# Seams of a four-layer graph network: six row buffers and deferred adds at the end of four-head attention, a routed layer's stores and row numbers, and other queues for readbacks

## The chip, the cores and the metric

The kernel runs on one core of a Trainium2 chip. The core has five engines that run side by side: TensorE (PE) multiplies matrices and transposes tiles, VectorE (DVE) and ScalarE (ACT) work element by element, GpSimd (POOL) does some setup and issues DMAs, SyncE (SP) issues DMAs. The metric is the device time of one launch in microseconds (us); lower is better.

## The reference, cut to what matters

A graph of 2,708 nodes with 256 features each passes through four layers. Each layer adds a graph step and a feed-forward step to X, each on the layer-normed X. All is fp32.

```python
x = x + L0_gnn(layernorm(x), adj, ...)   # cosine attention on the graph
x = x + L0_ffn(layernorm(x), ...)        # attention over slices
x = x + L1_gnn(layernorm(x), adj, ...)   # four-head graph attention
x = x + L1_ffn(layernorm(x), ...)        # eight experts, the best one per node
x = x + L2_gnn(layernorm(x), adj, ...)   # single-head graph attention
x = x + L2_ffn(layernorm(x), ...)        # a decoder block; two of its experts per node
x = x + L3_gnn(layernorm(x), adj, ...)   # single-head graph attention, ELU
x = x + L3_ffn(layernorm(x), ...)        # linear

def L1_gnn(x, adj, W, a1, a2):
    h = (x @ W).reshape(n, 4, 64)
    si, sj = einsum('nhd,d->nh', h, a1), einsum('nhd,d->nh', h, a2)
    e = where(adj > 0, leaky_relu(si[:, None] + sj[None], 0.2), -9e15)
    return einsum('ijh,jhd->ihd', softmax(e, axis=1), h).reshape(n, 256)

def L1_ffn(x, W1, b1, Wg, bg, Wd, bd):
    H = gelu(x @ W1 + b1)                      # 1,024 wide
    probs = softmax(H @ Wg + bg)               # 8 experts
    assign = argmax(probs)
    return sum over e of (assign == e) * probs[e] * (H @ Wd[e] + bd[e])
```

## The kernel before

The nodes lie in 22 tiles of 128 rows (the last has 20), X stays on the chip as 128 x 22 x 256, and a "block" is up to 512 nodes, four tiles; there are six blocks, the last of two tiles. `net_kernel` (L2014) calls the layers in turn. Most of the order on an engine follows from the order in which the code issues, with a scheduler between; `tc.issue_after(x)` pins an instruction behind another on its engine.

**Four-head attention**, `gat_heads` (L678). The heads go in two pairs. For each source tile j, ACT (L674) and DVE (L675) make the weights e of both heads against all nodes; TensorE adds values into six accumulators `acc` (L780, one PSUM bank each) and the sums of weights into `den` (L788, one bank). After the 22 tiles of a pair, DVE copies den to `ds` (L798), TensorE turns it (L801), DVE makes the reciprocals `rd` (L803, L806). Then, block by block, acc goes to a row buffer `o` of which there are three (L810, ACT and DVE in turn), is turned by TensorE into the one PSUM bank `aux` (L815), multiplied by rd (`y`, L822) and added to X (L829). `mark_empty` (L2049) loads two rows of flags into the mask by ACT's DMA queue (L2053, L2054), ahead of the pair loop.

**The top-1 layer**, `top1_ffn` (L857), has three stages.
- Its head: eight expert weights `wd` of 1 MB each are loaded by SP (L880), `ln_stats` takes layer norm's sums and roots for all tiles in groups of four (L96; a group is `bn_stats` L144, `bn_aggr` L145, ACT's square root L147, DVE's reciprocal L151), and w (1 MB, L892) comes by GpSimd's queue.
- Its hidden part, over the blocks: `features` (L894) norms and turns four tiles, `hidden` (L904) multiplies by w (L911) and applies GELU on ACT, `gate` (L932) computes logits and a rank for each node and lets GpSimd scatter each tile's 128 node numbers, four bytes each, into lists in DRAM called `fnodes` (L1444). `store` (L918) turns the hidden rows back (L926), copies them to row buffers `hr` (three, DVE and ACT in turn, L927) and lets SP write them to DRAM, `hidden` (L930). The stores of the last two blocks both follow the last gate.
- Its expert part: SP loads the node numbers as columns, 128 x 8 for the first eight tiles (L1554, `load_first`) and 128 x 1 for each later one (L1550, `load`); DVE casts them to integers (L980); GpSimd fetches each tile's rows of `hidden` (L990); TensorE turns them (L1003) and multiplies by wd (L1035); the result goes out by GpSimd (`send`, L1573).

`Routing.combine` (L1583) reads the experts' results back into y by SP's and ACT's queues in turn (L1594) and adds them to X (L1604). It runs at the start of the single-head layer and of the last graph layer, whose mask `reload_graph` (L2057) clears by GpSimd and loads again by SP, with `mark_empty` behind it.

Of the kernel before, what the change touches and what calls it, by code (L numbers as in the profile page):

```python
# [677 lines left out]
def gat_heads(net):  # L678
# [8 lines left out]
    Q = len(cols) // 2  # L687
    with ExitStack() as ctx:
        big = ctx.enter_context(tc.tile_pool(name="g1big", bufs=1))
        V = big.tile([P, NT, H, DH], F32, name="V")  # L690
        ratio = big.tile([P, NT, H], F32, name="ratio")

        low = big.tile([P, NT, H, 2 * Q - 1], F32, name="low")
        big_p = big.tile([P, H, N], F32, name="big_p")
# [73 lines left out]
        for p in range(2):  # L768
# [3 lines left out]
            nc.tensor.matmul(den, zero, big_p[0:1, 0, :512], start=True, stop=False, skip_group_check=True)  # L772
            for j in range(NT):
                e = wide.tile([P, 2, N], F32, name="e")
                for k, h in enumerate(heads):
                    gat_pairs(net, e[:, k, :], j, 0, N, big_p[:, h, :], ratio[:, j, h : h + 1])
                for n, (i0, iw) in enumerate(cols):
                    for k, h in enumerate(heads):
                        half = slice(k * DH, (k + 1) * DH)
                        nc.tensor.matmul(  # L780
                            acc[n][half, :iw], V[:, j, h, :], e[:, k, i0 : i0 + iw], start=j == 0, stop=j == NT - 1
                        )
                for q in range(Q):
                    for k, h in enumerate(heads):
                        for half in range(2):
                            i0, iw = cols[half * Q + q]
                            g = (2 * k + half) * 32
                            nc.tensor.matmul(  # L788
# [6 lines left out]
                            )  # L795

            ds = small.tile([P, 512], F32, name="ds", bufs=1)
# [4 lines left out]
            rd = small.tile([P, 4, 4, Q], F32, name="rd", bufs=1)  # L802
# [4 lines left out]
            out = []  # L807
            for n, (i0, iw) in enumerate(cols):
                o = small.tile([P, 512], F32, name="o", bufs=3)
                (nc.vector.tensor_copy if n % 2 else nc.scalar.copy)(o[:, :iw], acc[n][:, :iw])  # L810
                pt = paux.tile([P, 4, P], F32, name="aux")
                its = tiles_of(i0, iw)
                for c, i in enumerate(its):
                    r = rows(i)
                    nc.tensor.transpose(pt[:r, c, :], o[:, c * P : c * P + r], net.ident)  # L815
                whole = [c for c, i in enumerate(its) if rows(i) == P]
                for c0, c1, r in [(0, len(whole), P)] + [(c, c + 1, rows(its[c])) for c in range(len(whole), len(its))]:
                    nt = c1 - c0
                    y = small.tile([P, 4, 2, DH], F32, name="y")

                    d = rd.rearrange("p c (k b) q -> p c k b q", b=2)[:r, c0:c1, :, n // Q, n % Q]
                    nc.vector.tensor_tensor(  # L822
                        y[:r, :nt],
                        pt[:r, c0:c1, :].rearrange("p c (k d) -> p c k d", d=DH),
                        d.unsqueeze(3).to_broadcast([r, nt, 2, DH]),
                        ALU.mult,
                    )
                    xs = X[:r, its[0] + c0 : its[0] + c1, p * 2 * DH : (p + 1) * 2 * DH]
                    nc.vector.tensor_tensor(xs, xs, y[:r, :nt].rearrange("p c k d -> p c (k d)"), ALU.add)  # L829
# [27 lines left out]
def top1_ffn(net, ctx):  # L857

    nc, tc, a, X = net.nc, net.tc, net.a, net.X
    E, HID = 8, 1024
    KC = HID // P
    with ExitStack() as inner:
        big = ctx.enter_context(tc.tile_pool(name="f1big", bufs=1))
        dram = ctx.enter_context(tc.tile_pool(name="f1dram", bufs=1, space=bass.MemoryType.DRAM))
        wd = inner.enter_context(tc.tile_pool(name="f1wd", bufs=1, side="right")).tile([P, E, KC, D], F32, name="wd")
# [11 lines left out]
        for e in range(E):  # L879
            nc.sync.dma_start(wd[:, e], a["f1_wd"][e].rearrange("(c p) m -> p c m", p=P))  # L880
        route = Routing(net, big, dram, 1, "f")
        ln = net.ln_stats()
# [3 lines left out]
        with tc.tile_pool(name="f1tp", bufs=2, space=PSUM) as ptp, tc.tile_pool(  # L886
# [7 lines left out]
            def features(its):  # L894
                ft = work.tile([P, 2, 512], F32, name="ft")
                for k, t in enumerate(its):
                    r = rows(t)
                    f = rp.tile([P, D], F32, name="f", bufs=2)
                    net.normed(f, t, ln)
                    ps = net.transposed(ptp, f, r)  # L900
                    nc.vector.tensor_copy(ft[:, :, k * P : k * P + r], ps[:, :, :r])
                return ft

# [14 lines left out]
            def store(its, halves):  # L918

                for k, t in enumerate(its):  # L920
                    r = rows(t)
                    for n, half in enumerate(halves):
                        hr = rp.tile([P, 512], F32, name="hr", bufs=3)
# [3 lines left out]
                        (nc.scalar.copy if n else nc.vector.tensor_copy)(  # L927
# [21 lines left out]
            blocks, kept = chunks(512), []  # L949
            ft = features(tiles_of(*blocks[0]))  # L950
            for n, (n0, nw) in enumerate(blocks):
                its = tiles_of(n0, nw)
                halves = hidden(ft, nw)
                if n + 1 < len(blocks):
                    ft = features(tiles_of(*blocks[n + 1]))
                gate(its, halves, nw)
                kept.append((its, halves))
                if n + 2 != len(blocks):
                    for k in kept:
                        store(*k)  # L960
                    kept.clear()
        route.finish()
        prep = ctx.enter_context(tc.tile_pool(name="g2prep", bufs=1))
        with tc.tile_pool(name="f1t", bufs=1, space=PSUM) as pt, tc.tile_pool(
# [5 lines left out]
            node, number, to = (  # L970
                sp.tile([P, route.tiles], t, name=name, bufs=1)
                for t, name in ((F32, "node"), (I32, "number"), (I32, "to"))
            )
# [40 lines left out]
            for s in range(E, usual):  # L1014
                route.load(s, node[:, s : s + 1])
# [1143 lines left out]
```

## Time and profile before

| | us |
|---|---|
| median of three runs (2892.7 to 2900.67) | 2898.42 |
| the profiled execution | 2896.45 |
| its span | 2894.7 |
| four-head attention, from den of the first pair's first tile (707.75) to the last pair's last den (1070.06) | 362.3 |
| from there to the first matmul of the hidden part, L911 (1095.19) | 25.1 |
| hidden part to the first expert matmul (1251.88) | 156.7 |
| last store of `hidden` issued | 1231.8 |
| last graph layer: readbacks issued (2576.82) to TensorE's first transposes (2597.47) | 20.7 |

The times in brackets are microseconds from the start of the span. The profile's page gives each engine's busy time; the window view gives, for a stretch, the busy time of each engine with its instruction count, TensorE's granted clock (1.00 is full), the share of the DMA engines in use and the GB/s that they moved. A timeline line is the start, the duration, the engine (with a q for the engine's DMA-issuing queue) and line, the operation, what it writes and reads, and in square brackets how long the engine had been idle before it and what released it. A waits line gives engine and instruction, what it waited for, the total, the number of waits and the longest.

### The profile page before, as it was taken

The page shows a single profiled execution, that of the slowest core. Times are in us where ns is not written, and L with a number is a line of the kernel's source. Part 1 is how long each engine was busy: PE and PEld are TensorE (multiplying, and loading weights), DVE is VectorE, ACT ScalarE, POOL GpSimd, SP SyncE. Part 2 cuts the span into 40 slices and gives each one's busy share as a digit, 9 for nine tenths or more (in the row PEclk, how much of TensorE's full clock was granted, in tenths as well). Part 3 has the DMA queues.
Part 4 walks back from the last instruction along what each step waited for, and adds up shares of the span by engine and source line. Part 5 has one row for each costly group of instructions (what it writes and reads, how often), then busy time and mean ns, then how long its engine had stood idle before and what let it go on. Part 6 is the DMA issues. An engine that isn't in the chain of part 4 may idle for free. (4 is left out here: it accounts for less than half of the span.)

```text
span 2894.7 us, 32765 instructions
## 1 busy us (share of the span) xinstructions
PE 2651.2 (92%) x11893; PEld 1624.4 (56%) x11893; DVE 1441.4 (50%) x3062; ACT 1041.2 (36%) x1658; POOL 369.5 (13%) x462
## 2 busy tenths in 40 slices
PE   6999989799999989878899899998979999969998
PEld 5667746563333334567688433333346677747885
DVE  7753358344777774432644455455543222235455
ACT  3344433224665643211543223233312222215453
POOL 0000012100000001133300123223321111110002
PEclk9999999698999998989999999899969999989999
DMA  8899210000000005354200100002021111041001
GB/s 298 280 292 312 104 65 1 8 1 1 1 1 1 1 19 173 91 166 130 87 1 0 34 22 17 15 0 93 15 101 41 34 30 34 28 137 59 1 1 39
DMA packets 113729, 197.70 MB, mean 68 GB/s; under 512 B 12380, under 2 KB 71636, under 8 KB 110732
## 3 DMA queue, kind: packets, MB, share of 16 engines
q1 hardware_dynamic: 92758, 147.89, 16.1%
q0 software_dynamic: 13120, 38.06, 4.0%
q10 hardware_dynamic: 7690, 9.62, 1.1%
q8 instruction: 99, 1.62, 0.2%
q14 instruction: 62, 0.51, 0.1%
HBM read 135.82 MB, written 59.71 MB: 68 GB/s over the span
## 5 line engine op out<-in xcount | busy, mean ns | idle before, releaser
L675 DVE SCALAR_TENSOR_TENSOR e<-e,mask 128x768 f32<-128x768 f32 (+2 forms) x264 | 411.7, 1574 | 310.9 <-ACT e L674 310.7
L674 ACT ACTIVATE e<-big_p,minus_one,ratio 128x768 f32<-128x768 f32 (+2 forms) x264 | 394.9, 1513 | 363.4 <-PE acc L1236 229.8
L1236 PE MATMUL acc<-V,e 128*128 128x257 f32 (+1 forms) x1936 | 433.5, 383 | 4.5 <-DVE e L675 4.4
L1236 PEld LDWEIGHTS acc<-V,e 128*128 128x128 f32 (+1 forms) x1936 | 352.3, 186 | 85.7 <-issue 32.1
L780 PE MATMUL acc<-e,V 128*64 128x512 f32 (+1 forms) x1056 | 249.7, 550 | 4.1 <-DVE e L675 4.1
L1878 PE MATMUL h<-w,ft 128*128 (+1 forms) x752 | 233.0, 452 | 0.5 <-ACT ft L1860 0.5
L284 PE MATMUL acc<-F,e 128*128 128x257 f32 x968 | 226.3, 384 | 3.3 <-DVE e L281 2.9
L284 PEld LDWEIGHTS acc<-F,e 128*128 128x128 f32 x968 | 173.4, 185 | 67.3 <-DVE e L281 28.7
L780 PEld LDWEIGHTS acc<-e,V 128*64 128x64 f32 x1056 | 95.4, 137 | 180.6 <-issue 159.0
L1719 PE MATMUL sc<-qt,kt 64*128 64x512 f32 (+4 forms) x656 | 187.0, 535 | 4.1 <-ACT e L1729 2.4
L1729 ACT ACTIVATE e<-sc 128x1024 f32<-128x1024 f32 (+4 forms) x140 | 102.8, 760 | 204.5 <-PE sc L1719 188.4
L1878 PEld LDWEIGHTS h<-w,ft 128*128 128x128 f32 x752 | 136.0, 191 | 56.7 <-issue 1.4
L281 DVE TENSOR_TENSOR e<-e,mask 128x512 f32<-128x512 f32 (+2 forms) x132 | 80.4, 625 | 149.4 <-ACT e L275 147.8
L1737 DVE TENSOR_TENSOR sum<-sum,e 128x1024 f32<-128x1024 f32 (+4 forms) x102 | 103.8, 1018 | 99.1 <-ACT e L1729 97.4
L275 ACT ACTIVATE e<-score 128x512 f32<-128x512 f32 (+2 forms) x132 | 69.7, 544 | 179.2 <-PE score L273 153.0
L1734 PE MATMUL po<-e,V 128*64 128x512 f32 (+5 forms) x560 | 119.4, 511 | 14.8 <-ACT e L1729 8.8
L1910 PE MATMUL po<-w,ht 114*128 (+1 forms) x564 | 129.5, 379 | 0.9 <-DVE ht L1903 0.9
L1719 PEld LDWEIGHTS sc<-qt,kt 64*128 64x128 f32 x656 | 71.8, 198 | 94.8 <-issue 80.9
L788 PE MATMUL den<-e,low 128*3 128x512 f32 (+1 forms) x1056 | 123.1, 542 | 0.0
L1910 PEld LDWEIGHTS po<-w,ht 114*128 114x128 f32 x564 | 106.7, 189 | 22.6 <-DVE ht L1903 8.2
L1563 DVE TENSOR_SCALAR second<-f,down 128x1 f32<-128x1 f32 x47 | 10.0, 213 | 213.6 <-DMA f<-hs 213.6
L273 PE MATMUL score<-QK 128*128 128x512 f32 (+2 forms) x264 | 112.1, 554 | 1.2 <-ACT e L275 0.7
(605 smaller groups left out, 3501.0 us busy)
## 6 DMA issues: line engine op xcount, KB each, us to landing
row<-in_adj SPq DMA_DIRECT2D x21, 1354.0 KB
raw<-in_adjT SPq DMA_DIRECT2D x35, 768.0 KB
hs<-zero SPq DMA_DIRECT2D x8, 2838.0 KB
hidden<-hr SPq DMA_DIRECT2D x42, 256.0 KB
wd<-in_f_wd SPq DMA_DIRECT2D x8, 1024.0 KB
kept<-mask SPq DMA_DIRECT2D x21, 338.5 KB
mask<-kept SPq DMA_DIRECT2D x21, 338.5 KB
f<-hs SPq DMA_DIRECT2D x47, 129.0 KB
```

What stands on the lines that cost most here:

```text
L273: nc.tensor.matmul(ps[:r, :iw], QK[:, 0, span(j)], QK[:, 1, i0 : i0 + iw], start=True, stop=True)
L284: nc.tensor.matmul(acc[k][:ri], e[:r, k * P : k * P + ri], F[:r, j, :], start=j == 0, stop=j == NT - 1)
L674: nc.scalar.activation(v, big_p[:, i], AF.Relu, bias=net.minus_one, scale=ratio)
L675: return nc.vector.scalar_tensor_tensor(v, v, 1.0, net.mask[:, j, i], ALU.add, ALU.mult)
L780: nc.tensor.matmul(acc[n][half, :iw], V[:, j, h, :], e[:, k, i0 : i0 + iw], start=j == 0, stop=j == NT - 1)
L788: nc.tensor.matmul(den[g : g + Q, :iw], low[:, j, h, Q - 1 - q : 2 * Q - 1 - q], e[:, k, i0 : i0 + iw], start=False, stop=j == NT - 1 and ...
L1236: nc.tensor.matmul(acc[k][:ri], e[:, k * P : k * P + ri], V[:, j, :], start=j == 0, stop=j == NT - 1)
L1719: nc.tensor.matmul(ps[:r, g, o:iw], kt[b, span(j)], qt[b, o:iw], start=True, stop=True)
L1734: nc.tensor.matmul(po[b, o:iw], V[:r, j, g, :], e[:r, g, o:iw], start=j == 0, stop=j == last)
L1737: (nc.gpsimd if part else nc.vector).tensor_tensor(total, total, e[:r, :, o:iw], ALU.add)
L1878: last = nc.tensor.matmul(halves[s, n][:, q, :HALF], fts[s][:, c, :], weights.w13[n][:, es[s], c, q * HALF : (q + 1) * HALF], start=c == 0 ...
L1910: last = nc.tensor.matmul(po, ht[:KP, k, :], w2[:KP, es[s], k, :], start=k == 0, stop=k == KC - 1)
```

## The change

Each name below is as in the diff.
- `gat_heads` takes a pool `keep` with all six `o` blocks and the reciprocals of both pairs. In a pair's last source tile, den's matmuls are issued before the values, and each step's order is pinned. The adds of the first pair stay; those of the second are handed back as a function.
- `top1_ffn` calls `gat_heads` and runs the second pair's adds itself, through its own two PSUM banks `tp`. Ahead of the first features come add 0, sums of block 0, add 1 and the roots; behind them sums of block 1, add 2, sums of block 2 and `newton` (an inverse root by DVE alone) for both blocks. Adds 3 to 5 with their sums and their newton come inside block 0, after the features of block 1 and ahead of its gate. All these are pinned one behind another.
- `wd` is loaded by GpSimd's queue, after the last add, in the memory that `keep` leaves.
- The stores of the last two blocks copy on ACT only; the last but one writes into eight spare buffers, made of tiles that are free by then.
- Node numbers are loaded as rows of 128 numbers, one row for each expert tile, into three places of a tile; TensorE turns a group, and DVE casts it. The groups are 8, 9 and 9 tiles, where they were 8, 4, 4, 4, 4 and 2.
- `combine` uses SP and GpSimd in turn, and `mark_empty` uses GpSimd.

The matmuls and the elementwise work inside the pair loop are the same as before.

```diff
-def gat_heads(net):
+def gat_heads(net, keep):
...
+    o = keep.tile([P, len(cols), 4 * P], F32, name="o")
+    rds = [keep.tile([P, 4, 4, Q], F32, name=f"rd{p}") for p in range(2)]
+    def add(p, n, psum, tag):
+        i0, iw = cols[n]
+        its = tiles_of(i0, iw)
+        pt = psum.tile([P, 4, P], F32, name="aux", tag=tag)
+        for c, i in enumerate(its):
+            r = rows(i)
+            nc.tensor.transpose(pt[:r, c, :], o[:, n, c * P : c * P + r], net.ident)
+        y = o[:, n, :].rearrange("p (c k d) -> p c k d", c=4, k=2)
+        for c0, c1, r in whole_and_rest(its):
+            d = rds[p].rearrange("p c (k b) q -> p c k b q", b=2)[:r, c0:c1, :, n // Q, n % Q]
+            nc.vector.tensor_tensor(
+                y[:r, c0:c1],
+                pt[:r, c0:c1, :].rearrange("p c (k d) -> p c k d", d=DH),
+                d.unsqueeze(3).to_broadcast([r, c1 - c0, 2, DH]),
+                ALU.mult,
+            )
+            xs = X[:r, its[0] + c0 : its[0] + c1, p * 2 * DH : (p + 1) * 2 * DH]
+            last = nc.vector.tensor_tensor(xs, xs, y[:r, c0:c1].rearrange("p c k d -> p c (k d)"), ALU.add)
+        return last
...
+            last = nc.tensor.matmul(den, zero, big_p[0:1, 0, :512], start=True, stop=False, skip_group_check=True)
+            for j in range(NT):
+                e = wide.tile([P, 2, N], F32, name="e")
+                for k, h in enumerate(heads):
+                    gat_pairs(net, e[:, k, :], j, 0, N, big_p[:, h, :], ratio[:, j, h : h + 1])
+                for step in (values, weights) if j + 1 < NT else (weights, values):
+                    with tc.issue_after(last.ins):
+                        last = step(e, j)
...
             for n, (i0, iw) in enumerate(cols):
-                o = small.tile([P, 512], F32, name="o", bufs=3)
...
+                (nc.vector.tensor_copy if n % 2 else nc.scalar.copy)(o[:, n, :iw], acc[n][:, :iw])
+                if p == 0:
+                    add(p, n, paux, "aux")
+    return lambda n, psum, tag: add(1, n, psum, tag)
...
+        held = ExitStack()
+        add = gat_heads(net, held.enter_context(tc.tile_pool(name="g1keep", bufs=1, side="right")))
...
-        wd = inner.enter_context(tc.tile_pool(name="f1wd", bufs=1, side="right")).tile([P, E, KC, D], F32, name="wd")
...
-        for e in range(E):
-            nc.sync.dma_start(wd[:, e], a["f1_wd"][e].rearrange("(c p) m -> p c m", p=P))
...
-        ln = net.ln_stats()
+        stats = Stats(net)
+        ln = stats.mean, stats.rstd
...
-            def store(its, halves):
+            def store(its, halves, late=False, room=()):
+                room = list(room)
                 for k, t in enumerate(its):
                     r = rows(t)
                     for n, half in enumerate(halves):
-                        hr = rp.tile([P, 512], F32, name="hr", bufs=3)
+                        hr = room.pop(0) if room else rp.tile([P, 512], F32, name="hr", bufs=3)
                         ps = pg.tile([P, 4, P], F32, name=f"hr{n}")
                         for c in range(KC // 2):
                             nc.tensor.transpose(ps[:r, c, :], half[:, c, k * P : k * P + r], net.ident)
-                        (nc.scalar.copy if n else nc.vector.tensor_copy)(
+                        (nc.scalar.copy if n or late else nc.vector.tensor_copy)(
...
+            tiles = [(tiles_of(*b)[0], tiles_of(*b)[-1] + 1) for b in blocks]
+            turn(add, 0, ptp, "tp")
+            turn(stats.sums, *tiles[0])
+            turn(add, 1, ptp, "tp")
+            turn(stats.roots, *tiles[0])
             ft = features(tiles_of(*blocks[0]))
+            turn(stats.sums, *tiles[1], root=False)
+            turn(add, 2, ptp, "tp")
+            turn(stats.sums, *tiles[2], root=False)
+            turn(stats.newton, rp, tiles[1][0], tiles[2][1])
             for n, (n0, nw) in enumerate(blocks):
                 its = tiles_of(n0, nw)
                 halves = hidden(ft, nw)
                 if n + 1 < len(blocks):
                     ft = features(tiles_of(*blocks[n + 1]))
+                if n == 0:
+                    for m in range(3, len(blocks)):
+                        turn(add, m, ptp, "tp")
+                        turn(stats.sums, *tiles[m], root=False)
+                    turn(stats.newton, rp, tiles[3][0], NT)
+                    last = None
+                    held.close()
+                    wd = inner.enter_context(tc.tile_pool(name="f1wd", bufs=1, side="right"))
+                    wd = wd.tile([P, E, KC, D], F32, name="wd")
+                    for e in range(E):
+                        nc.gpsimd.dma_start(wd[:, e], a["f1_wd"][e].rearrange("(c p) m -> p c m", p=P))
                 gate(its, halves, nw)
                 kept.append((its, halves))
-                if n + 2 != len(blocks):
-                    for k in kept:
-                        store(*k)
-                    kept.clear()
+                if n + 2 < len(blocks):
+                    store(*kept.pop())
+            spare = [work.tile([P, 2, 512], F32, name="spare", tag="ft") for _ in range(2)]
+            spare.append(work.tile([P, KC // 2, 512], F32, name="spare", tag="ht512", bufs=3))
+            room = [t[:, k, :] for t in spare for k in range(t.shape[1])]
+            for k in kept:
+                store(*k, True, room)
+                room = ()
...
-            node, number, to = (
-                sp.tile([P, route.tiles], t, name=name, bufs=1)
-                for t, name in ((F32, "node"), (I32, "number"), (I32, "to"))
-            )
+            number, to = (sp.tile([P, route.tiles], I32, name=name, bufs=1) for name in ("number", "to"))
             usual = route.usual
-            groups = [range(E)] + [range(s, min(s + 4, usual)) for s in range(E, usual, 4)]
+            groups = [range(E)] + [range(s, min(s + 9, usual)) for s in range(E, usual, 9)]
+            rowed = sp.tile([P, P], F32, name="rowed", bufs=1)
             held = {}
-            def numbers(group):
+            def load(group, at):
+                node = rowed[at : at + len(group), :]
+                if group[0] == 0:
+                    route.load_first(node)
+                else:
+                    for k, s in enumerate(group):
+                        route.load(s, node[k : k + 1, :])
+            def numbers(group, at):
                 g = slice(group[0], group[-1] + 1)
-                nc.vector.tensor_copy(number[:, g], node[:, g])
-            def places(group):
+                here = slice(at, at + len(group))
+                ps = pt.tile([P, len(group)], F32, name="node", bufs=1)
+                nc.tensor.transpose(ps, rowed[here, :], net.ident[here, here])
+                nc.vector.tensor_copy(number[:, g], ps)
+                return ps
...
+                        for n, g in enumerate(groups):
                             if s + 6 == g[0]:
-                                numbers(g)
-                                places(g)
+                                places(g, numbers(g, 32 * n))
...
+        rows_of = self.hs[bass.ds(row, P), :]
+        self.loaded = sync.dma_start(f, rows_of.rearrange("p d -> d p") if self.choices == 1 else rows_of)
     def load_first(self, f):
         self.loaded = self.net.nc.sync.dma_start(
-            f, self.hs.rearrange("(e c) d -> c (e d)", e=self.E)[:P, :]
+            f, self.hs.rearrange("(e c) d -> e (c d)", e=self.E)[:, :P]
...
-                    (nc.sync, nc.scalar)[(n + c) % 2].dma_start(
+                    (nc.sync, nc.gpsimd)[(n + c) % 2].dma_start(
...
-    net.nc.scalar.dma_start(row[:, :whole], net.flags[:LAST])
-    net.nc.scalar.dma_start(row[:, whole:], net.flags[LAST:NT, : N - whole])
+    net.nc.gpsimd.dma_start(row[:, :whole], net.flags[:LAST])
+    net.nc.gpsimd.dma_start(row[:, whole:], net.flags[LAST:NT, : N - whole])
```

## The prediction

> **What bounds the kernel now.** I read the page's busy shares first, then the chain that ended last.
>
> ```profile
> PE 2651.2 (92%) x11893; PEld 1624.4 (56%) x11893; DVE 1441.4 (50%) x3062; ACT 1041.2 (36%) x1658; POOL 369.5 (13%) x462
> ...
> PE 18%; DMA 3%; DVE 2%; issue 1%; ACT 0%; POOL 0%; ACTq 0%; DVEq 0%; POOLq 0%
> ```
>
> TensorE is at work or stalled inside a matmul for 92% of the span, so time can be won only where it waits or crawls. The change touches no inner loop. The view by windows compares a steady stretch with the seams that the change does touch.
>
> ```profile
> core 0: us, PE busy (x) PEld busy (x) DVE busy (x) ACT busy (x) POOL busy (x), PEclk, DMA share, GB/s
> 698.90:878.90 180.00, 179.97 (x1056) 57.92 (x1056) 130.71 (x46) 114.34 (x46) 0.00 (x0) 0.98 0.00 1
> 878.90:914.00 35.10, 35.10 (x151) 11.40 (x150) 27.88 (x26) 16.13 (x7) 0.00 (x0) 1.00 0.00 0
> ...
> 1070.00:1095.20 25.20, 9.57 (x39) 5.45 (x37) 23.35 (x92) 3.65 (x8) 4.62 (x13) 0.56 0.61 184
> ...
> 1112.00:1133.40 21.40, 21.31 (x96) 11.26 (x95) 7.22 (x28) 7.74 (x12) 4.00 (x4) 1.00 0.27 99
> 1215.40:1251.90 36.50, 10.91 (x47) 7.83 (x48) 11.92 (x50) 4.55 (x7) 8.97 (x10) 0.51 0.66 157
> 2573.00:2597.50 24.50, 0.32 (x3) 0.06 (x1) 8.97 (x29) 1.95 (x3) 3.67 (x4) 0.61 0.83 261
> ```
>
> Row by row: four-head attention's first pair runs 1,056 matmuls in 180 us. The switch to the second pair has 151 in 35 us, so "100% busy" there is mostly waiting. The head of the top-1 layer (1070 to 1095) belongs to DVE. Its second block (1112 to 1133) is TensorE's. The end of its hidden part and the head of the last graph layer leave TensorE idle. The timeline gives the edges:
>
> ```profile
> 1070.14 0.69 DVE L798 COPY ds<-den 128x512 f32<-128x512 f32 x1 [4.85 <-PE den L788]
> ...
> 1095.19 6.22 PE L911 MATMUL h<-ft,w 128*128 128x512 f32 x8
> ...
> 1234.23 0.41 SPq L1554 DMA_DIRECT2D node<-fnodes  x1
> ...
> 1241.48 0.17 DVE L980 CAST number<-node 128x8 int32<-128x8 f32 x1 [6.20 <-DMA node<-fnodes]
> ...
> 2576.82 12.74 ACTq L1594 DMA_DIRECT2D y<-dys  x7
> ...
> 2595.07 1.28 ACT L147 ACT_TABLE_LOAD   x1 [21.37 <-DMA y<-dys]
> ...
> 2596.69 0.18 DVE L151 RECIPROCAL rstd<-sd 128x4 f32<-128x4 f32 x1 [6.37 <-ACT sd L147]
> ...
> 2597.47 1.73 PE L1134 MATMUL tp<-ident,f 128*128 128x128 f32 x7 [24.18 <-DVE f L108]
> ```
>
> The last four lines show ACT's queue full of readbacks: its square root, needed by DVE and then TensorE, sits behind seven DMA issues. The list of waits (1066 to 1260) names the row buffers of the hidden part:
>
> ```profile
> ACT hr L927 <- DMA hidden<-hr: 12.8, 7, 7.8
> ...
> DVE hr L927 <- DMA hidden<-hr: 8.5, 3, 4.0
> ```
>
> **What the Trainium skill says.** "DMA: Bandwidth & Descriptors", section "Issuing engines are not separate DMA queues": another issuing engine saves only sequencer time, the 16 engines being shared. The trace agrees: the eight expert parts moved at about 348 GB/s, one slice after another, with the engines full. So moving the readbacks frees ACT, not bandwidth, and moving the expert weights frees SP only. The same page, "Anatomy of one DMA — SWDGE (gpsimd) path", gives about 2.0 us fixed plus the bytes; here small GpSimd loads land in 2.0 to 2.9 us, 1 MB of w in 5.2. Its "Specifications" say that elements under 512 B cost a read-modify-write: here a 128x8 load of 4-byte elements takes 7 us, and the scatters of 128 four-byte numbers queue up. "TensorE: Matmul & The Clock Gate", "What's actually happening": an idle array falls to half clock; here the first eight matmuls after the gap took 6.22 us, later ones 0.43 each.
>
> **The change part by part**, in the clock of the profiled execution (2896.45 us, span 2894.7; the median of the runs shown is 2.0 higher).
>
> *Flags on GpSimd.* Two issues of 0.87 and 0.76 us leave ACT before the first e (691.2 to 692.95). ACT feeds that loop's start: **−0.7** (0 to −1.6).
>
> *Six o buffers at the pair switch.* From the end of den (878.97) to den of j=2 (914.00) are 35.0 us. A steady cycle is (876.29 − 707.75)/21 = 8.03 us; two cycles and the values of a third (8.03 − 2.75) are 21.3, the 28 transposes and the zeroing add 5.7: 27.0. So 8.0 us are stalls, because an o copy waits for a buffer whose transposes wait for the single aux bank. With six buffers the accumulators empty at once, and with den first in the last j the weights are ready 5.3 us sooner. But DVE has 25.5 to 28.5 us of work there (five to six e at 2.98, twelve y and X at 0.5 to 0.7, the copies), so it is late next, at about 28: **−7** (−3 to −9).
>
> *Head of the top-1 layer.* Today h starts 25.1 us after den's end (1070.06), behind all six adds, six groups of statistics, and DVE's clearing of small tiles. After: den ends at 1064.8 and ds is copied under the last values; from 1070.1 follow transposes of ds (0.7), rd and reciprocal (0.9), add 0 (transposes beside it, y 0.69, X 0.69) to 1073.1; statistics of four tiles 1.75 (as at 2585.35 to 2587.10); add 1, 1.4; root and reciprocal 0.3; features of block 0, four f at 0.38 and four copies at 0.39 plus 1.5 of hand-over, to 1081; add 2's transposes, 1.1, ahead on TensorE. h starts at 1082.2: **−13.0**. The next late thing is w: issued at 1073.89 behind the same wait, 5.2 to landing, about 1080; that cover is only 2 us. What is put off must be paid in block 0 (today 21.4 us from h's end to the next h's end): adds 3 to 5, 3.7; statistics of ten tiles, 4.4; twelve Newton steps of 0.2, 2.4: 10.5 us of DVE, issued ahead of the gate's chain to the ranks. DVE has 14 us free there, and 14 more while h runs (1095 to 1112, 2.41 busy), but TensorE's order puts the adds' transposes after h, so 0 if all lies beside TensorE, 10.5 if none: I take half, **+5.3**.
>
> *Expert weights on GpSimd's queue, late.* Today they cross at 1085 to 1110 beside nothing else. Afterwards they start with the last add and meet the hidden stores of two blocks (4.2 MB; together 12.6 MB, 36 us at 348 GB/s). Row buffers come free later: **+1.5** (0 to +4). Behind them on GpSimd stand the scatters of blocks 0 and 1, each waiting for a weight part's semaphore; nobody reads the scatters before 1228. Eight issues of 0.75 us are hidden there.
>
> *Spare rows and the tail.* The waits of the two fences go: twelve ACT copies of 0.59 are 7.1 us, so the last store is issued near 1222 instead of 1231.8. But the node load waits for all scatters too, and the last, issued 1218.65, lands 9.5 us later, about 1228.2 (six scatters land about 2.5 apart). So of 9.8 us 6.0 remain: 1234.23 to 1228.2.
>
> *Numbers as rows.* The load becomes eight rows of 512 B: 2.2 us (the smallest landing among today's loads of numbers), plus transpose and hand-over 0.7, against 7.25 to the cast: −4.4. Together with the spare rows **−10.4**; with stores that share less and scatters at 1223, −16; with scatters held at their place and a load of 5 us, −4.
>
> *Readbacks.* At the last graph layer the sums of block 0 are ready at 2587.1 and DVE, after the second add (2590.3), waits 6.37 us. With ACT free the root is done by 2588.5: **−6.3** (−2, if GpSimd's first readback lands late or its 2.35 us mask clearing gets in front, to −6.4). At the single-head layer ACT did not stall (root at 1376.0 just after the add's 1372.6): **0** (−0.5 to +1.5, seven GpSimd issues of 0.75 to 1 us with 4.5 to landing). In mark_empty of the last layer the two flag DMAs leave ACT too, counted in the 6.3.
>
> Sum: −0.7 − 7 − 13.0 + 5.3 + 1.5 − 10.4 − 6.3 + 0 = **−30.6**: 2896.45 − 30.6 = **2866**. All best: −1.6 − 9 − 13 − 16 − 6.4 − 0.5 = −46.5, 2850. All worst: −3 − 13 + 10.5 + 4 − 4 − 2 + 1.5 = −6, 2890.
>
> **Rivals.**
> *Given back* (chance 0.19): DVE's chain in block 0 is a chain indeed (+10.5), the weights slow the stores (+3), the switch gives 5, the tail 7, readbacks 4: −0.7 − 5 − 13 + 10.5 + 3 − 7 − 4 = −16.2, **2880**. For it: DVE is the head's owner (23.35 of 25.2), and TensorE waits for the gate's ranks in order. Against it: DVE's 7.22 busy of 21.4.
> *Better* (0.17): stalls vanish, the deferred work hides (+1), scatters land sooner: −0.7 − 8.5 − 13 + 1 − 15 − 6.4 = −42.6, **2854**. For it: 14 idle us of DVE in block 0.
> *It does not do what it says* (0.04): fixed orders and two tp banks keep the head as long as before, and only tail and readbacks gain: −10.4 − 6.3 + 5.3 + 1.5 = −9.9, **2887**. Against it: no buffer of o is left to wait for.
> *Slower* (0.04): the weights starve on GpSimd's queue. They are issued about 1102 and the eighth part is used by the eighth tile, near 1244 (in this clock, earlier gains taken off), 142 us later. Below 8.39 MB/142 us = 59 GB/s expert matmuls wait; below 46 GB/s the wait exceeds 39 us, all gains and 0.3%. At 40 GB/s they land at 1312, 68 late: 2866 + 68 − 10 (other tail work hidden under it) = **2924**. Against it: 3.4 MB of the slice layer's weights, issued by GpSimd, landed within 13.2 us, and GpSimd's issues take 0.72 to 0.99 us beside DVE copies.
>
> **How the numbers follow.** Forecast 0.56, better 0.17, given back 0.19, no effect 0.04, slower 0.04. One run can tell 0.3% (8.7 us) from nothing: faster is under 2889.7. The range leaves out the slow case, no-effect and the tails of the two neighbours: 2848 to 2884. Faster 0.92 (the first three), same 0.04 (no effect, which lies 3 us from the bound), slower 0.04.
>
> **What would show it.** In the profile after: den of the second pair's j=2 about 28 us after the first pair's last matmul, not 35; first h 12 us after the accumulators' end, not 25; from h's end to the second block's about 27, not 21; SP's node load issued 6 us after the last store lands or the last scatter, and its cast 3 us later, not 7; no ACT wait for y<-dys at the last layer, and its first transposes 6 us sooner. Wrong if the weights are what the expert matmuls wait for, or DVE's ranks stretch block 0 by 10 us or more, or the gain at the switch stays under 3.

## The result and the profile after

| | before | after |
|---|---|---|
| median of 20 runs, us | 2895.80 | 2887.89 |
| lowest to highest | 2889.15 to 2900.67 | 2875.97 to 2895.76 |
| ratio, 95% interval | | 0.9973 [0.9964, 0.9982] |
| profiled execution / its span | 2896.45 / 2894.7 | 2884.84 / 2883.0 |

The change gains 7.9 us where 30.6 were forecast; 2887.89 lies above the stated range (2848 to 2884). That it lands beside the 2887 of the rival "It does not do what it says" is chance: that rival has the head as long as before, and the head got 14 us shorter. The page's first and fourth part say little: busy times agree within a per cent but for GpSimd's. The chain is followed for the whole span this time (its shares add up to 100%, before to 24%), so the two can't be compared.

```profile
PE 2650.7 (92%) x11896; PEld 1640.9 (57%) x11896; DVE 1439.8 (50%) x3066; ACT 1042.4 (36%) x1659; POOL 385.9 (13%) x485
...
PE 75%; DVE 9%; DMA 6%; issue 4%; ACT 4%; POOL 2%; ACTq 0%; POOLq 0%; SPq 0%; DVEq 0%
```

The edges that the prediction named, in the timeline after:

```profile
1057.88 0.69 DVE L836 COPY ds<-den 128x512 f32<-128x512 f32 x1 [2.85 <-PE den L816]
...
1073.56 4.52 PE L943 MATMUL h<-ft,w 128*128 128x512 f32 x8
...
1228.24 0.28 SPq L1620 DMA_DIRECT2D rowed<-fnodes  x1
...
1231.45 0.17 DVE L1048 CAST number<-node 128x8 int32<-128x8 f32 x1 [1.48 <-PE node L1047]
...
2571.09 4.91 POOL L1660 DMA_DIRECT2D y<-dys  x7 [0.75 <-DMA dys<-y,to]
...
2582.31 0.30 ACT L147 ACTIVATE sd<-mv,ln_eps 128x4 f32<-128x4 f32 x1 [12.88 <-DVE mv L145]
2585.34 0.17 DVE L151 RECIPROCAL rstd<-sd 128x4 f32<-128x4 f32 x1
2586.10 1.73 PE L1199 MATMUL tp<-ident,f 128*128 128x128 f32 x7 [18.98 <-DVE f L108]
```

den is ready 4.7 us ahead of the values' end (1062.5), and h, the first matmul of the hidden part, follows 11.1 us after that end, not 25.1. From the node load to the cast are 3.2 us, not 7.25. At the last graph layer the square root now waits for DVE's statistics and for no readback. All of this is as forecast. So h starts 21.6 us earlier on this clock (1095.19 to 1073.56). But the first expert matmul comes only 11.4 us earlier (1251.88 to 1240.5). The gain is given back in between. The window view by blocks of the hidden part (a block ends with its last GELU) shows where:

```profile
core 0: us, PE busy (x) PEld busy (x) DVE busy (x) ACT busy (x) POOL busy (x), PEclk, DMA share, GB/s
1062.40:1073.50 11.10, 4.81 (x26) 3.38 (x25) 10.00 (x40) 2.13 (x3) 4.48 (x13) 0.78 0.36 106
1073.50:1089.00 15.50, 15.11 (x36) 6.50 (x35) 7.05 (x30) 5.99 (x8) 0.00 (x0) 0.94 0.00 0
1089.00:1117.20 28.20, 25.51 (x112) 13.27 (x111) 17.32 (x75) 7.53 (x12) 9.23 (x10) 0.94 0.54 194
1117.20:1154.30 37.10, 29.39 (x109) 15.57 (x111) 10.02 (x36) 8.43 (x13) 5.81 (x6) 0.82 0.81 193
1154.30:1176.90 22.60, 22.60 (x104) 12.02 (x100) 9.50 (x35) 7.74 (x12) 3.87 (x4) 1.00 0.26 94
```

The rows are the head, then blocks 0 to 3. This is block 2 in the kernel before:

```profile
1134.30:1156.90 22.60, 22.60 (x106) 12.03 (x101) 9.61 (x35) 7.85 (x12) 3.87 (x4) 1.00 0.26 94
```

Block 2 of the changed kernel (1117.20) makes about as many matmuls (109 and 106) in 37 us instead of 23, and its DMA share is 0.81 instead of 0.26. The DMA view of 1103 to 1143 in the changed kernel tells what moves (40 slices of 1 us; the two q lines are GpSimd's and SP's queue):

```profile
DMA  0459999999999999999999999999999969997306
GB/s 0 53 152 299 342 352 381 385 414 397 414 367 373 391 391 352 356 336 352 356 340 348 348 346 387 399 404 399 371 279 217 29 31 78 96 94 60 85 3 236
...
q0 software_dynamic: 2432, 8.39, 61.0%
q1 hardware_dynamic: 1411, 2.60, 32.1%
...
wd<-in_f_wd POOLq DMA_DIRECT2D x8, 1024.0 KB, 16.0
hidden<-hr SPq DMA_DIRECT2D x10, 256.0 KB
```

A block of the kernel before (1134 to 1157) has only its stores there, with gaps on both sides:

```profile
DMA  0000000000796000978092570059910000000000
...
hidden<-hr SPq DMA_DIRECT2D x8, 256.0 KB
```

The weights fill the engines for some 25 us while the rows of blocks 0 and 1 are due. The timeline of the changed kernel shows how that reaches TensorE:

```profile
1122.31 0.59 ACT L961 COPY hr<-hr 128x512 f32<-128x512 f32 x1 [4.23 <-PE hr L960]
...
1122.92 22.31 SPq L964 DMA_DIRECT2D hidden<-hr  x8
...
1126.41 0.59 ACT L961 COPY hr<-hr 128x512 f32<-128x512 f32 x1 [0.52 <-PE pr L977]
...
1140.95 0.59 ACT L961 COPY hr<-hr 128x512 f32<-128x512 f32 x1 [12.89 <-DMA hidden<-hr]
...
1141.59 1.11 PE L960 MATMUL hr<-ident,ht 128*128 128x128 f32 x4 [4.30 <-ACT hr L961]
```

ACT has no free row buffer until a store lands (12.89 us), TensorE's next transposes wait for ACT, and the h matmuls stand behind them in order. SP needs 22.31 us for this block's eight stores, 10.12 before.

### The profile page after: what moved, and what is told of

Its sections match the earlier page's. It is cut to its first block, busy times and chain, and to the rows that moved or that the text cites. A ratio compares the mean times of both kernels' runs of the same rounds, so it can differ in the third digit from the quotient of the medians.

```text
span 2883.0 us, 32763 instructions
## 1 busy us (share of the span) xinstructions
PE 2650.7 (92%) x11896; PEld 1640.9 (57%) x11896; DVE 1439.8 (50%) x3066; ACT 1042.4 (36%) x1659; POOL 385.9 (13%) x485
## 4 chain that ended last, share of the span: by engine, by line
PE 75%; DVE 9%; DMA 6%; issue 4%; ACT 4%; POOL 2%; ACTq 0%; POOLq 0%; SPq 0%; DVEq 0%
PE acc L1301 15%; PE acc L805 8%; PE acc L284 7%; PE den L816 4%; PE po L1976 4%; PE po L1800 4%; PE sc L1785 4%; PE score L273 3%; PE h L1944 3%; PE pv L123 3%; DMA f<-hs 2%; PE h L943 2%; PE po L123 2%; PE sc L1763 2%; PE y L1103 1%
## 5 line engine op out<-in xcount | busy, mean ns | idle before, releaser
L805 PE MATMUL acc<-e,V 128*64 128x512 f32 (+1 forms) x1056 | 242.7, 548 | 4.4 <-DVE e L675 4.4
L805 PEld LDWEIGHTS acc<-e,V 128*64 128x64 f32 x1056 | 107.9, 137 | 161.8 <-issue 129.2
L1976 PEld LDWEIGHTS po<-w,ht 114*128 114x128 f32 x564 | 106.7, 189 | 22.6 <-DVE ht L1969 8.2
```

Source lines behind the costliest of these rows:

```text
L805: made = nc.tensor.matmul(acc[n][half, :iw], V[:, j, h, :], e[:, k, i0 : i0 + iw], start=j == 0, stop=j == NT - 1)
L1976: last = nc.tensor.matmul(po, ht[:KP, k, :], w2[:KP, es[s], k, :], start=k == 0, stop=k == KC - 1)
```

## Experiments

Theory A: the burst of weights, where it meets stores that are due, costs what I priced at 1.5 us. Rival B: the software queue itself, with the scatters behind the weights. Rival C: the deferred adds, statistics and fixed orders. All runs below are the changed kernel with one edit; times from the traces are in this table. Blocks are from last GELU to last GELU, and "cast" is the first cast of node numbers. Each ratio is to the kernel before as it ran beside that run.

| us | block 1 | block 2 | block 3 | block 4 | last GELU to cast | first h to first expert matmul | median, ratio to before |
|---|---|---|---|---|---|---|---|
| before, three traces | 21.3 to 21.6 | 22.5 to 22.6 | 22.6 | 22.5 to 22.6 | 30.9 to 32.2 | 155.4 to 156.7 | |
| after, three traces | 26.6 to 28.4 | 36.2 to 39.1 | 22.5 | 22.6 | 24.7 to 25.4 | 166.9 to 169.3 | 0.9973 [0.9964, 0.9982] |
| wd_spread | 26.0 | 29.5 | 29.1 | 27.3 | 24.5 | 169.2 | 2889.07, 0.9973 [0.9964, 0.9983] |
| wd_spread, second trace | 26.2 | 32.5 | 27.6 | 27.2 | 25.9 | 172.3 | |
| wd_sp | 23.7 | 41.9 | 21.6 | 21.5 | 25.0 | 167.5 | 2887.35, 0.9968 [0.9954, 0.9983] |
| head_before | 21.3 | 22.6 | 22.6 | 22.6 | 24.5 | 146.8 | 2884.45, 0.9953 [0.9936, 0.9971] |
| wd_gap | 23.7 | 31.1 | 27.6 | 27.5 | 25.5 | 168.6 | 2886.15, 0.9960 [0.9942, 0.9978] |
| wd_after | 23.7 | 25.5 | 23.3 | 22.6 | 25.2 | 154.0 | 2874.75, 0.9935 [0.9916, 0.9954] |
| wd_after, second trace | 23.7 | 27.9 | 24.7 | 22.6 | 25.2 | 157.4 | |
| wd_burst_after | 23.7 | 47.4 | 20.9 | 21.5 | 25.7 | 172.7 | 2894.10, 0.9992 [0.9981, 1.0003] |
| no_spare | 28.5 | 37.4 | 22.6 | 22.6 | 27.1 | 171.3 | 2889.05, 0.9966 [0.9952, 0.9980] |
| cols | 28.2 | 36.3 | 22.6 | 22.6 | 28.7 | 172.0 | 2890.70, 0.9982 [0.9972, 0.9992] |
| act_queue | 26.6 | 39.3 | 22.6 | 22.6 | 25.0 | 169.4 | 2894.33, 0.9984 [0.9974, 0.9993] |

The medians can't price a single step. The end of the decoder's attention, which none of these edits touches (see More traces), took 163.3 us in the changed kernel's traces, but 152.0 in that of no_spare, 158.0 in that of act_queue and 149.7 in both of wd_after. So the steps are read from the stages of the traces.

**Weights two at a time, behind the last GELU of blocks 0 to 3.** A one-element copy by GpSimd from the block's last GELU into each part holds the load back.

```diff
-                    for e in range(E):
-                        nc.gpsimd.dma_start(wd[:, e], ...)
+                if n < 4:
+                    for e in (2 * n, 2 * n + 1):
+                        nc.gpsimd.tensor_copy(wd[0:1, e, 0, 0:1], halves[1][0:1, KC // 2 - 1, 0:1])
+                for e in range(2 * n, min(2 * n + 2, E)):
+                    nc.gpsimd.dma_start(wd[:, e], ...)
```

> The changed kernel, but the eight expert weights go out two at a time, each pair behind the last GELU of one of the blocks 0 to 3, instead of all eight in block 0. Theory A (the burst of 8.4 MB fills the DMA engines while the row stores of blocks 0 and 1 are written, and the three row buffers pass that on to TensorE): the third block, 37.1 us in the changed kernel (1117.2 to 1154.3), falls to 22.5 to 25, each block is at most 2 us longer than 22.5, the first expert matmul comes 10 to 13 us earlier against the first h, and the time is 18 to 21 us under the kernel before. Theory B (weights issued by GpSimd hold the scatters behind them on the same queue, wherever they are placed): the loss stays, spread over the blocks, and the time is within 4 us of the changed kernel.

Block 2 fell from 37 to 29.5, but blocks 3 and 4 rose to 29.1 and 27.3. The way from the first h to the first expert matmul is as long as with the burst. As it stood, A had expected the opposite, B this. Yet the last GELU is just where a block's stores begin, so each pair met stores again; the run speaks against A's "burst", not against A's "meets".

**Weights by SP's queue, at the same place.**

```diff
-                        nc.gpsimd.dma_start(wd[:, e], ...)
+                        nc.sync.dma_start(wd[:, e], ...)
```

> The changed kernel, but the eight expert weights are issued by SP's queue, at the same place in block 0. Theory A (bandwidth, whoever issues): the loss stays; the stores that SP issues behind the weights wait in the same queue, so blocks 0 to 2 together are as long as in the changed kernel (65.3 us from the end of the first h group to the end of the third block's) or up to 10 us longer. Theory B (GpSimd's queue is the cause): the third block falls to 23 to 25 us, and the time is about 10 us under the changed kernel.

Blocks 1 and 2 take 65.6 us together (changed kernel 64.5 to 65.8): the loss doesn't need GpSimd's queue, and B falls in this form. The Trainium skill says ("DMA: Bandwidth & Descriptors", "Issuing engines are not separate DMA queues") that DMAs share the same 16 DMA engines whichever engine issues them; this pair of runs agrees with it in the cost. But the way to the loss isn't quite the same: here SP sends no store between 1104.5 and 1132.2, because its own queue is busy with the weights.

**The head as before, the rest as changed.**

```diff
-                if p == 0:
-                    add(p, n, paux, "aux")
+                add(p, n, paux, "aux")
...
+        for e in range(E):
+            nc.sync.dma_start(wd[:, e], ...)
...
-        stats = Stats(net)
-        ln = stats.mean, stats.rstd
+        ln = net.ln_stats()
```

> The changed kernel with six o buffers and den first, spare rows, row numbers and readbacks as changed, but the second pair's adds and all of layer norm's statistics ahead of the hidden part again, and the weights issued by SP at its start, as in the kernel before. Theory A: h starts 13 to 15 us later than in the changed kernel, but the second block falls from 28.2 to 21.4 us and the third from 37.1 to 23.4, so the first expert matmul comes 5 to 8 us earlier and the time is 13 to 17 us under the kernel before: deferring as it was done costs more than it gives. Rival C (the third block is slow for another reason of the new order, such as the deferred statistics or the fixed orders): also gone here, so this run alone doesn't tell A from C, but together with the spread weights it does.

Every block is that of the kernel before. From den's last start to h are 28.7 us, 12.3 more than in the changed kernel, and the first expert matmul comes 20 us sooner after h. So the deferral as it was done, with the late weights that belong to it, costs more than it gives. It is the traces that show this: in the times (12 us under the kernel before by the medians, 14 by the ratio) the intervals of the two ratios overlap.

**Weights in pairs behind the fourth GELU.** The edit is that of the spread weights, moved into `hidden`: `if k == 3 and 1 <= n <= 4`.

> The changed kernel, but the expert weights go out by GpSimd's queue two at a time behind the fourth GELU of the blocks 1 to 4: that is where a block's row stores have been written and TensorE runs 9 us of plain h matmuls. Theory A2, formed after the spread weights lost 29.1 us in all, not less than the burst: bytes of the weights that move while row stores are due hold these back for as long as they take, 6 us for each 2 MB at 350 GB/s, wherever the block; three row buffers can't bridge that. Then here blocks 2 to 4 take 22.5 to 23.5 us, block 1 no more than 26, the first expert matmul comes 150 to 155 us after the first h (changed kernel 166.9), and the time is 20 to 25 us under the kernel before. Theory B (GpSimd's queue, the semaphores that scatters and weights share): the loss stays, 5 to 7 us in each of four blocks, and the time is that of the changed kernel within 4 us.

Blocks 2 to 4 took 27.5 to 31.1: a miss. The timeline of GpSimd in this run tells why:

```profile
1139.62 0.97 POOL L1513 DMA_INDIRECT fnodes<-ftag,fto  x1 [0.30 <-issue]
1140.60 0.30 POOL L951 COPY wd<-ht 1x1 f32<-1x1 f32 x2
1141.07 1.86 POOL L953 DMA_DIRECT2D wd<-in_f_wd  x2 [0.17 <-POOL wd L951]
```

The pair stands behind four scatters and goes out at 1141, 4.5 us before the block's end (1145.6), so it moved beside the next block's stores (the first of them is issued at 1150.43). The gap was missed.

**Weights in pairs behind the row stores, by SP.**

```diff
+                        sent = nc.sync.dma_start(rows_of[span(t), n * 512 : (n + 1) * 512], hr[:r])
+                return sent
...
+                    sent = store(*kept.pop())
+                    with tc.issue_after(sent.ins):
+                        for e in range(2 * n, 2 * n + 2):
+                            nc.sync.dma_start(wd[:, e], ...)
```

> The changed kernel, but the expert weights go out by SP's queue, two at a time, pinned behind the last row store of each of the blocks 0 to 3. In the trace of the run behind the fourth GELU the pairs were issued after the block's scatters, 22 us into the block, and moved while the next block's rows were due; here they should move in the 9 us in which TensorE runs plain h matmuls. Theory A2 (weights cost time only where they move beside row stores that are due): blocks 2 to 4 take 22.5 to 23 us each, block 1 takes 23.5 to 24.5 (the deferred adds alone), the first expert matmul comes 148 to 151 us after the first h (changed kernel 166.9), and the time is 15 to 19 us under the changed kernel. Rival G (2 MB of weights cost a block 5 us wherever they are put, by memory or by the queue): blocks 2 to 4 take 27 to 28 us as in that run, and the time is within 4 us of it.

Now the pairs hit the gap, as SP's timeline shows, and the windows of blocks 1 to 4 (1.00 is full clock) have the bytes in them, most of them without the time:

```profile
1121.51 12.95 SPq L964 DMA_DIRECT2D hidden<-hr  x8
1134.51 1.19 SPq L1015 DMA_DIRECT2D wd<-in_f_wd  x2
1147.04 10.31 SPq L964 DMA_DIRECT2D hidden<-hr  x8
1157.40 1.20 SPq L1015 DMA_DIRECT2D wd<-in_f_wd  x2
```

```profile
1091.60:1115.30 23.70, 23.70 (x111) 12.90 (x110) 16.52 (x75) 7.74 (x12) 2.72 (x3) 1.00 0.38 127
1115.30:1140.80 25.50, 22.95 (x101) 11.87 (x100) 9.37 (x34) 7.84 (x12) 5.18 (x6) 1.00 0.63 154
1140.80:1164.10 23.30, 22.93 (x101) 11.87 (x100) 9.28 (x34) 7.74 (x12) 3.87 (x4) 1.00 0.69 190
1164.10:1186.70 22.60, 22.60 (x101) 12.02 (x100) 9.37 (x34) 7.74 (x12) 3.88 (x4) 1.00 0.75 188
```

The last row has a DMA share of 0.75 and 188 GB/s, twice block 3 of the changed kernel (0.26, 94), and takes the same 22.6 us. 154.0 us from h to the first expert matmul is 3 above the expectation, since block 2 keeps 3 us; DVE still waits 3.50 us there for a store to land. A second trace gave 157.4, with 5.3 us left in block 2 and 2.1 in block 3; that of the spread weights gave 172.3. So the placement takes away 12 to 15 of the 19 us that the weights cost the changed kernel, not all. Rival G falls with blocks 3 and 4, and C falls too, since all deferred work is in this run: it costs 2.3 us in block 1. This version beats both kernels, 0.9935 [0.9916, 0.9954], 19 us under before, but only 11 under the changed kernel by the ratios, where 15 to 19 were expected. And not all of the 19 is the placement: in its two traces 8 us against the kernel before are the end of the decoder's attention.

**All eight behind the stores of block 0, by SP.**

```diff
-                        for e in range(2 * n, 2 * n + 2):
+                        for e in range(E if n == 0 else 0):
```

> The same, but all eight weights go out by SP behind the last row store of block 0. Theory A2: 3 of 8.4 MB fit in the 9 us that are free, 5.4 MB move while the stores of block 1 are due and hold them for 5.4 MB at 350 GB/s, 15 us; these stores follow in the same queue, so the block that holds them takes 37 to 40 us and the others 22.5. The first expert matmul comes 13 to 16 us later than with the pairs behind the stores. Rival G: the loss is 18 to 20 us, as in the changed kernel.

It lost 18.7 us against the first trace of the pairs, above A2's 13 to 16 and in G's range, though G had fallen; against their second trace it is 15.3, inside A2's. SP's timeline has what I left out:

```profile
1099.49 11.69 SPq L964 DMA_DIRECT2D hidden<-hr  x8
1111.54 26.07 SPq L1015 DMA_DIRECT2D wd<-in_f_wd  x8
1137.71 37.23 SPq L964 DMA_DIRECT2D hidden<-hr  x15
```

Issuing eight parts held SP for 26 us, and block 1's first store, copied at 1121.1, left at 1137.71.

**Single parts undone.** Row copies and spare rows (`store(*k)` for `store(*k, True, room)`):

> The changed kernel without spare rows and without copies on ACT alone for the last two blocks (three row buffers, DVE and ACT in turn). My prediction's step: the waits for row buffers come back, the last store is issued 4 to 9 us later, and, since the scatters land in between, the first expert matmul comes 4 to 6 us later. Rival E: the last stores are bound by bytes (twelve stores of 256 KB are 9 us at 350 GB/s) and not by buffers, so the cast comes within 2 us of where it is in the changed kernel (24.8 us after the last GELU).

From the last GELU, the cast comes 1.8 to 2.5 us later than in the three traces of the changed kernel, the last store 2.1 us later than in the first, and the first expert matmul 1.9 to 2.9: the step's sign holds, but it is worth about 2 us and not 4 to 6, so this is nearer to rival E. Columns for rows (the old `load`, `numbers` and both DMA forms):

> The changed kernel with node numbers loaded as columns again (groups of 8, 9 and 9). My prediction's step: the load to the cast takes 7.25 us instead of about 3, so the first expert matmul comes 4.4 us later and the time is 4 us above the changed kernel. Rival D: the first fetch is held by something else (the last stores) and the cast comes later anyway, so the time is within 1.5 us of the changed kernel.

From the last GELU, the cast comes 3.3 to 4.0 us later and the first expert matmul 4.1 to 5.1; the step holds. Readbacks and flags on ACT (`nc.scalar` for `nc.gpsimd` in `combine` and `mark_empty`):

> The changed kernel with readbacks and flags on ACT's queue again. My prediction's step: the last graph layer's first transposes come 5 to 6.4 us later (26.2 instead of 21.1 us after the decoder's last expert matmul), four-head attention starts 0.7 to 2 us later, and the time is 6 us above the changed kernel. Rival F: the last graph layer's head is bound by the readbacks' bytes anyway and the shift is under 2 us.

From the decoder's last expert matmul to the last layer's first values are 26.0 us instead of 21.1, and the way from the last matmul ahead of the flags to the first den 17.4 instead of 15.5 to 16.9. The step of the readbacks holds. That of the flags is small against its spread: the kernel before has 17.0 to 17.4.

**More traces.** The end of the decoder's attention, from its last key matmul to its last score matmul, differs between kernels that are the same there. Six single runs give more traces: the kernel before (2896.52 and 2895.58 us), the changed one (2893.78 and 2892.15), the spread weights (2896.57) and the pairs behind the stores (2867.38).

> The kernel before once more, for a second trace. In the first traces the end of the decoder's attention, which no part of the change touches, took 157.7 us before and 163.3 after, with TensorE's granted clock falling to half at another point. If that is the luck of the clock, this run shows another value than 157.7 (152 to 164); if it is the change's doing, it shows 157.7 again. All other stages should agree with the first trace within 0.7 us.

> The changed kernel once more, for a second trace. The end of the decoder's attention took 152.0, 157.7 to 158.0, or 163.3 us in ten traces of kernels that are the same there. If that is the clock's luck in each execution, this trace may show any of the three; if a program always has its own value, it shows 163.3 again. The stages of the top-1 layer should agree with the first trace within 1 us (blocks 28.3 and 36.2).

> The changed kernel, third trace. Theory P (the clock's course at the end of the decoder's attention follows from the program's own timing, so it repeats): 163.2 to 163.4 us there. Theory L (luck of the execution): another of the values seen, 149.7 to 158.

> The kernel before, third trace. Theory P: 157.5 to 158.1 us at the end of the decoder's attention. Theory L: another of the values seen.

> The weights spread behind the last GELU of each block, second trace. Theory P: 152.0 us at the end of the decoder's attention. Theory L: any of the values seen. The blocks 1 to 4 repeat 26.0, 29.5, 29.1 and 27.3 us within 1.5.

> The weights in pairs behind the row stores, second trace. Theory P: 149.7 us at the end of the decoder's attention. Theory L: any of the values seen. The blocks 1 to 4 repeat 23.7, 25.5, 23.3 and 22.6 us within 1.

Three traces of the kernel before gave 157.7, 158.0 and 157.7 us, three of the changed one 163.3, 163.2 and 163.3, both of the pairs behind the stores 149.7. But the spread weights gave 152.0 and then 164.7. So the value mostly repeats with a program, yet not always: theory P holds in three of the four tests, and neither theory explains all. Other stages repeated less well than expected: the way from the last GELU to the first expert matmul within 1.2 us in the second trace of the kernel before (0.7 expected), blocks within 2.9 us in the changed kernel (1 expected), 2.9 with the spread weights (1.5 expected) and 2.3 with the pairs (1 expected). Two equal slices up to the same point of the work, before and then after:

```profile
2100.00:2120.00 20.00, 18.51 (x152) 12.23 (x152) 10.20 (x31) 6.68 (x17) 3.23 (x4) 0.94 0.00 1
2120.00:2140.00 20.00, 19.88 (x91) 11.92 (x90) 6.47 (x26) 4.17 (x10) 7.30 (x8) 0.50 0.08 27
```

```profile
2094.50:2114.50 20.00, 19.36 (x108) 12.85 (x110) 7.10 (x25) 4.29 (x11) 1.80 (x3) 0.62 0.00 1
2114.50:2134.50 20.00, 19.87 (x90) 11.96 (x90) 6.49 (x26) 4.18 (x10) 7.30 (x8) 0.50 0.08 28
```

TensorE's granted clock falls to half shortly before these last 20 us in one and some 13 us sooner in the other: the slice ahead of them holds 152 matmuls against 108. No part of the change touches this stage. Why the fall comes where it comes wasn't settled.

## Why the prediction was wrong

The table has means over three traces of each kernel (the pair switch and the head are from the first traces):

| step | forecast | measured |
|---|---|---|
| flags on GpSimd | −0.7 | −1.3 (17.3 to 16.0) |
| pair switch | −7 | −4.5 (362.3 to 357.8 from first den to last matmul) |
| head | −13.0 | −14.0 (25.1 to 11.1) |
| block 0 at a better clock | 0 | −1.2 (17.7 to 16.5) |
| deferred adds and statistics | +5.3 | +2.3 (21.4 to 23.7, block 1 where no weights meet its stores) |
| **expert weights** | **+1.5** | **+19.1** (block 1 27.8 for 23.7, block 2 37.5 for 22.5) |
| spare rows and row numbers | −10.4 | −7.5 (last GELU to first expert matmul, 41.7 to 34.2) |
| readbacks | −6.3 | −5.0 (26.0 to 21.1) |
| decoder's clock | 0 | +5.5 |
| sum | −30.6 | −6.6 (spans 2894.5 to 2888.5; medians −7.9) |

The step that failed is the one on the expert weights: "Row buffers come free later: **+1.5** (0 to +4)". It had the right traffic in it (12.6 MB, 36 us at 348 GB/s) and then put a price on the stores' lateness without working out how long a store may be late. A block's eight stores share three row buffers, and TensorE's order puts the next h matmuls behind the transposes that wait. So the time in which weights move beside due stores counts nearly in full: 19.1 of the 24 us that 8.4 MB take at 348 GB/s. That the placement makes most of the loss is shown by the pairs behind the stores: the same bytes and the same deferred work as in the changed kernel, in the same queue as the two runs with all weights by SP, which lost as much or more. The spread pairs show that a smaller burst alone doesn't help. Two things weren't tried: pairs that really move in the gap by GpSimd's queue, and more row buffers, so it isn't shown that more buffers would bridge the wait. My chance for "given back" was 0.19, with the right place but 3 us for the stores and 10.5 for DVE; DVE's chain came to 2.3. My sign "from h's end to the second block's about 27" came out at 26.6 to 28.4, but by luck: some 4 us of it are the weights.

The second error is in the tail. I had the scatters land last, with the last store near 1222. The last scatter landed at 1226.39, and the last store was copied at 1225.93 after ACT had waited 9.50 us for a row buffer: the last block's four row copies had three buffers, and the change's eight spare ones go to the block ahead of it. From the last GELU to the node load the change gained 3.5 us (25.0 to 21.5), not 6. The remaining 5.5 us are the decoder's clock, which nothing in the profile of before could give me. The mechanisms of switch, head, row numbers and readbacks were right, and the flags' gain is too small to judge; the switch was over-estimated by 2.5 us (from the first pair's last matmul, 876.0, to den of j=2 are 30.2 us and not 28; DVE waited 3.51 and 2.27 us there for transposes into the one bank `aux`), and the readbacks by 1.3, as DVE's adds of the first block waited for a readback in their midst (2.43 us, to 2578.06).

## What to carry to other kernels

A transfer that nobody waits for isn't free: ask which short, due transfers it runs beside, and how many buffers these have. Without slack, count nearly its full time (here 19.1 of 24 us). Put bulk loads in the stretch in which the DMA row shows zeros, behind the last due store on the same queue (here 3.8 to 7.4 us were left of the 19.1), and read in the timeline that they went there: a trigger alone isn't the place, since whatever stands ahead in the queue comes first.

## What the runs showed of the hardware

- Eight 1 MB loads kept SP's queue busy issuing for 26.07 us (3.3 each), about as long as 8.4 MB take at 348 GB/s (24 us); two took 1.2 us. GpSimd issued the eight in 7.17 us. SP's weights travel in small packets (10,912 for 13.11 MB with the stores), GpSimd's in larger ones (2,432 for 8.39 MB).
- TensorE's granted clock fell to 0.50 with the engine 19.9 of 20 us busy in the trace. The same work took 149.7 to 164.7 us in different traces; where it took 163.3 and not 157.7, the clock had fallen 13 us sooner.
